# Second cross-attention and feed-forward of a two-block transformer: program order in one pool, inverses by way of DRAM, one row spread to 64 partitions by each transfer

## The chip, the cores and the metric

The kernel runs on one core of a Trainium2 chip. TensorE (PE) multiplies matrices into PSUM; VectorE (DVE), ScalarE (ACT) and GpSimd (POOL) do elementwise work; SyncE (SP), and ACT in a few places, issue DMA transfers. Each engine executes its own instructions in order and waits on semaphores for the others. The metric is device time in microseconds of one execution, lower is better.

## The reference

Two blocks work on x of shape 8 x 512 x 256 (batches, tokens, features), all in float32, with a conditioning vector per batch and 64 context tokens of 192 features per batch. The first block has a self-attention with 16 heads of 16, a cross-attention and a gated feed-forward. The second block, cut to what matters here:

```python
attn_in = adaln(x, cond, ...)                  # layer norm, then (1+g) and b from cond
x = attn(attn_in, attn_in, sa_wq, sa_wkv, sa_wo, sa_bo) + x     # 16 heads of 64
cross_in = adaln(x, cond, ...)                 # the same g and b as above
x = attn(cross_in, layernorm(context), ca_wq, ca_wkv, ca_wo, ca_bo) + x
ffn_in = adaln(x, cond, ...)
x = gelu(ffn_in @ ff_w1 + ff_b1) @ ff_w2 + ff_b2 + x            # 256 -> 1024 -> 256
```

`attn` projects queries, keys and values, rotates queries and keys (RoPE), takes softmax(q k / 8) v for each head and projects by the output matrix.

## The kernel before, in words

All eight batches' x stay in SBUF, 128 tokens to a partition group, four groups to a batch. The program runs in phases; this change touches the last three, those of the second block.

*Self-attention (pool `ph4`).* Its order on PE, DVE, ACT and POOL is the order in which the code is written (`manual_schedule`). For each batch there are four groups of four heads, and for each group four slots, one for each 128 keys: `score` multiplies and ACT takes the exponential, `value` multiplies by v one slot later. POOL and DVE add the exponentials over the key tiles (`sm`). At the end of a group `sums` adds them over partitions by matmuls; ACT copies the denominators, they go to DRAM and come back as 128 x 16 (`sums_back`); `inverse` takes the reciprocal on DVE and writes it to DRAM; `inverse_back` (L950) reads two rows at a time to 128 partitions, each to 64, and `scaled` (L955) multiplies the head outputs `oT`. `out_tiles` projects them. These transfers go by SP, those of the last group of the last batch by ACT. In that last group's tail the values of the cross-attention (`cross_values`, eight matmul pairs, ACT copies v, SP writes it to DRAM in `v_d`) fill PE between the steps of the inverses. A batch takes 123.7 us.

*Cross-attention (pool `ph5`).* Here the framework's scheduler sets the order on each engine, from the dependences and the order of the code as priority; it can also move work up between instructions of the phase before. Each batch has eight pairs of heads and four blocks of two pairs. `norm` makes the normed rows, transposes them (L366, eight 128 x 128 transposes and two ACT copies) and adds the output bias to x (POOL, L380). `context` loads the batch's keys and values from DRAM into block-diagonal tiles `kb` and `vb` (six transfers). `outer` multiplies values by the output matrix beforehand, giving `vw`. `queries` multiplies, and `rope_pair` rotates: DVE at L720 and twice at L723, POOL adds at L724. `score` multiplies two pairs into one tile of two PSUM banks, and ACT takes the exponential to `p`. After four blocks, `sums` adds over the keys into one bank; DVE takes the reciprocal there of 128 x 512 (L1091), four transfers write the 16 needed rows to DRAM (L1095), and eight transfers (L1101) spread them, each two rows to 64 partitions; POOL and DVE in turn multiply `p` by them (L1104). Two blocks later the projection of `p` by `vw` adds to x.

*Feed-forward (pool `ph6`).* Also in the scheduler's order. The rows of each batch are normed and transposed; `ff_w1` in 32 matmuls (L1155 has the GELU on ACT), `ff_w2` in 64, DVE adds to x (L396), and SP stores the batch. Before the first batch a check over all reciprocals (`chk`, collected by `check`, L150) is reduced to one flag `good`, by which a general path is taken if the fast one is not safe.

*PSUM.* Eight banks: two tiles `S` of two banks each, two `X`, one `O`, one `D`. `bank_x` gives every third tile from `D` in the first block; from the second block's self-attention on (`turns.clear()`) it gives only the two `X`.

*What a norm is.* `layernorm` takes statistics on DVE (L187, L188; four pairs a batch), POOL raises to the power -1/2 (L179), DVE scales (L191).

All matmuls stand under line 107, in the helper `mm`; each of the program's float32 matmuls is two instructions in the trace.

Of the kernel before, what the change touches and what calls it, by code (L numbers as in the profile page):

```python
# [18 lines left out]
P = 128  # L19
# [59 lines left out]
def fast_path(ctx: ExitStack, tc: tile.TileContext, a: dict, out: bass.AP):  # L79
# [8 lines left out]
    turns = [0]  # L88
# [10 lines left out]
    def bank_x():  # L99
        if turns:  # L100
            turns[0] += 1
            if turns[0] % 3 == 0:
                return bank_d()
        return psum.tile([P, 512], F32, tag="X", name="ps_X", bufs=2)

# [268 lines left out]

    def normed_T(pool, x, b, eps, am, bm, bufs=2):
        return transposed(pool, normed(pool, b, eps), b, am, bm, bufs)
# [335 lines left out]
    k_d = dram.tile([B, P, NPAIR, T], F32, name="k_d", bufs=1)  # L712
    v_d = dram.tile([B, P, NPAIR, T], F32, name="v_d", bufs=1)
# [23 lines left out]
    def keys1(p):  # L737
# [6 lines left out]
        nc.sync.dma_start(k_d[:, :, p, :].rearrange("b r t -> r b t"), q.rearrange("p (b t) -> p b t", b=B))  # L744
# [56 lines left out]
    turns.clear()  # L801
# [9 lines left out]
    def load_kb(b):  # L811
        for i in range(4):
            r = slice(32 * i, 32 * i + 32)
            nc.sync.dma_start(kvs[b % 2][0][r, :, i % 2, :], k_d[b, r])

    def load_vb(b):
        for e in range(2):
            r = slice(64 * e, 64 * e + 64)
            nc.sync.dma_start(kvs[b % 2][1][r, :, e, :], v_d[b, r])
# [5 lines left out]
    def cross_values(wk, p):  # L825
        ps = bank_x()
        for k in range(2):
            mm(ps, cross["v"][:, k, p * P : (p + 1) * P], ctxzT[:, k, :], k == 0, k == 1)
        v = wk.tile([P, N], F32, tag="k0", name="v")
        nc.scalar.copy(v, ps)  # L830
        nc.sync.dma_start(v_d[:, :, p, :].rearrange("b r t -> r b t"), v.rearrange("p (b t) -> p b t", b=B))


    with tc.tile_pool(name="ph4", bufs=2) as wk:
        NG = H // 4
        kb, vb = kv_first()
        steps, mid = {}, {}
# [4 lines left out]
        def batch4(b):  # L842
# [103 lines left out]
            def inverse_back(g):  # L946
                d = s["inv", g]
                for u in range(2):
                    s["rb", g, u] = rb = wk.tile([P, N], F32, tag="rb", name="rb", bufs=3)
                    queue(g).dma_start(rb, d[2 * u : 2 * u + 2, None, :].to_broadcast([2, 64, N]))  # L950
# [51 lines left out]
        def slots():  # L1002
# [14 lines left out]
            sums(NG - 1)  # L1017
            for p in range(NPAIR):
# [4 lines left out]
            load_vb(0)  # L1023
            for qp in range(2):
# [5 lines left out]
    w_co, w_cq, rope_s2 = cross["o"], cross["q"], cross["s"]  # L1030


    with tc.tile_pool(name="ph5", bufs=2) as wk:
        kvs.append(tuple(wk.tile([P, NPAIR, 2, T], F32, name=n, bufs=1) for n in ("kb", "vb")))
        for z in kvs[1]:
            nc.gpsimd.memset(z, 0.0)

        w_f1 = load_w("ff_w1", 1)
        w_f2 = load_w("ff_w2", 3)
        blocks = []  # L1040

        def batch5(b):
            s = {}

            def norm():
                s["hT"] = transposed((nk, wk)[b % 2], normed(nk, b, EPS1), b, a1, b1, 1)
                add_row(b, row("cabo"))

            def context():
                s["kb"], s["vb"] = kvs[b % 2]  # L1050
                if b:
                    load_kb(b)
                    load_vb(b)

            def outer(pp):

                if pp == 0:
                    s["vw"] = wk.tile([P, NPAIR, D], F32, tag="vw", name="vw", bufs=3)
                ps = bank_x()
                for i in range(2):  # L1060
                    p = 2 * pp + i
                    mm(ps[:, i * D : (i + 1) * D], s["vb"][:, p, :, :].rearrange("p e k -> p (e k)"), w_co[:, p, :])
                nc.scalar.copy(s["vw"][:, 2 * pp : 2 * pp + 2, :], ps.rearrange("p (i d) -> p i d", i=2))

            def queries(p):
                ps = bank_x()
                for k in range(2):
                    mm(ps, w_cq[:, k, p * P : (p + 1) * P], s["hT"][:, k, :], k == 0, k == 1)
                s[p] = q = wk.tile([P, N], F32, tag="q", name="q", bufs=6)
                rope_pair(wk, ps[:, None, :], rope_c[:, None, :], rope_s2[:, None, :], [P, 1, N], q[:, None, :])  # L1070

            def block(pp):
                def score():
                    ps = bank_s()
                    for i in range(2):
                        p = 2 * pp + i
                        mm(ps[:, i, :], s["kb"][:, p, :, :].rearrange("p e k -> p (e k)"), s[p])
                    s["p", pp] = wk.tile([P, 2, N], F32, tag="p", name="p", bufs=8)
                    nc.scalar.activation(s["p", pp], ps, AF.Exp, scale=HD1 ** -0.5)

                return Block([score], [])

            def sums():

                d = bank_d()
                for i in range(2):
                    for j in range(4):
                        p = 4 * i + j
                        mm(d[32 * j : 32 * j + 32, :], sel3[:, i, :], s["p", p // 2][:, p % 2, :], i == 0, i == 1)
                rec = wk.tile([P, N], F32, tag="rec", name="rec", bufs=1)  # L1090
                nc.vector.reciprocal(rec, d)  # L1091
                rd = dram.tile([NPAIR, 2, N], F32, tag="rec5", name="rec5")
# [934 lines left out]
```

## Time and profile before

| | us |
|---|---|
| median of 3 runs (2522.51 to 2525.21) | 2523.86 |
| the profiled execution's own time | 2522.38 |
| its span, first to last instruction | 2520.5 |
| PE busy in the span | 2437.0 (97%) |
| DVE, ACT, POOL busy | 1095.1, 871.3, 850.9 |
| first matmul of the cross-attention after the last output tiles of the self-attention | 1907.3 |
| feed-forward's first matmul | 2281.1 |

The span is that of the profiled execution. Times in the text are microseconds from its start. "PE busy" counts a matmul from its start to the modelled end of its pipeline, so that consecutive ones overlap. A wait in square brackets behind an instruction is the time that its engine was idle before it, and the instruction that ended this. A transfer is issued by an engine's queue (SPq, ACTq) and lands later; the chain of waits shows transfers under DMA.

### The profile page before, as it was taken

To read this page: it belongs to the slowest core of one execution; us is meant where nothing else is said; L and a number is where in the kernel's file an instruction comes from. 1 tells how busy PE (TensorE), PEld (TensorE's weight loads), DVE (VectorE), ACT (ScalarE), POOL (GpSimd) and SP (SyncE) were. 2 spreads that over 40 slices of the span, in tenths; PEclk is the share of its full clock that TensorE was granted. 3 is DMA by queue.
4 is the path that set the end of the run, shared out by engine and by line. 5 is a ranking of instruction groups with operands and counts; after the bars stand their busy time and mean duration, and the time that the engine had idled before them with its cause. 6 is when DMAs were issued, how large, how long until landed. Compare 5 with 4: busy or idle time off the path is not lost.

```text
span 2520.5 us, 27970 instructions
## 1 busy us (share of the span) xinstructions
PE 2437.0 (97%) x10938; PEld 1152.9 (46%) x10938; DVE 1095.1 (43%) x2039; ACT 871.3 (35%) x1099; POOL 850.9 (34%) x521
## 2 busy tenths in 40 slices
PE   8999999999999899999999999999989999999999
PEld 3333443443445533434343434343435456556665
DVE  4555435435435334343444434445326765652000
ACT  3555546545542133242424243333232111112221
POOL 3453222322300035353535353536324434431000
PEclk9999999999999999999999999999999999999999
DMA  5130000000002000000000000000131321320000
GB/s 180 35 95 9 16 17 10 16 11 12 12 11 88 0 4 28 18 18 18 19 18 18 18 18 18 18 18 18 51 92 40 79 49 42 76 68 9 17 17 26
DMA packets 91084, 83.76 MB, mean 33 GB/s; under 512 B 51104, under 2 KB 67424, under 8 KB 90936
## 3 DMA queue, kind: packets, MB, share of 16 engines
q1 hardware_dynamic: 90388, 81.34, 11.0%
q8 instruction: 88, 1.44, 0.2%
q10 hardware_dynamic: 556, 0.55, 0.1%
q14 instruction: 52, 0.43, 0.1%
HBM read 72.09 MB, written 9.77 MB: 32 GB/s over the span
## 4 chain that ended last, share of the span: by engine, by line
PE 87%; DVE 4%; DMA 3%; issue 2%; POOL 2%; ACT 2%; SPq 0%; DVEq 0%; POOLq 0%; ACTq 0%
PE ps_X L107 42%; PE ps_S L107 22%; PE ps_D L107 11%; PE ps_O L107 9%; PE ps_X L366 1%; DMA rb<-rec_d 1%; DVE t L723 1%; ACT p L505 1%; POOL q L724 1%; DMA rb<-rec 1%; DVE t L720 1%; DVE st L187 1%; PE ps_X L485 0%; POOL p L1104 0%; PE ps_X L527 0%
## 5 line engine op out<-in xcount | busy, mean ns | idle before, releaser
L107 PE MATMUL ps_S<-q,k 32*128 32x512 f32 (+1 forms) x3072 | 432.5, 628 | 7.0 <-ACT p L505 3.4
L892 ACT ACTIVATE p<-ps_S 128x1024 f32<-128x1024 f32 x256 | 248.4, 1022 | 526.6 <-PE ps_S L107 519.1
L505 ACT ACTIVATE p<-ps_S 128x1024 f32<-128x1024 f32 x256 | 248.2, 1022 | 259.7 <-PE ps_S L107 258.8
L107 PEld LDWEIGHTS ps_S<-q,k 32*128 32x128 f32 (+1 forms) x3072 | 160.6, 185 | 245.7 <-issue 136.4
L871 DVE TENSOR_TENSOR t<-ps_X,rope_c 128x512 f32<-128x512 f32 x126 | 87.1, 691 | 341.0 <-PE ps_X L107 341.0
L911 DVE TENSOR_TENSOR sm<-sm,p 128x1024 f32<-128x1024 f32 x128 | 192.3, 1546 | 55.6 <-ACT p L892 54.3
L396 DVE TENSOR_TENSOR x<-ps_X,x 128x512 f32<-128x512 f32 x48 | 33.2, 692 | 342.6 <-PE ps_X L107 342.6
L874 POOL TENSOR_TENSOR q<-t 128x512 f32<-128x512 f32 x32 | 40.7, 1273 | 384.2 <-DVE t L872 384.2
L107 PE MATMUL ps_X<-hT,w 128*128 128x512 f32 x344 | 160.6, 601 | 1.6 <-DVE t L678 1.1
L907 POOL TENSOR_TENSOR sm<-p 128x1024 f32<-128x1024 f32 x64 | 149.2, 2353 | 32.5 <-ACT p L892 32.5
L724 POOL TENSOR_TENSOR q<-t,t 128x512 f32<-128x512 f32 x72 | 97.2, 1353 | 159.0 <-DVE t L723 151.3
L107 PE MATMUL ps_O<-p,h 128*32 128x512 f32 x1024 | 138.1, 612 | 0.5 <-ACT oT L518 0.5
L107 PE MATMUL ps_O<-p,v 128*64 128x512 f32 x512 | 138.0, 617 | 0.0
L107 PE MATMUL ps_D<-p,v 128*64 128x512 f32 x512 | 131.6, 592 | 1.1 <-ACT p L892 1.1
L179 POOL TENSOR_TENSOR rstd<-rstd,mhalf 128x4 f32<-128x4 f32 x49 | 49.6, 1015 | 241.4 <-DVE rstd L178 239.3
L107 PE MATMUL ps_X<-vw,p 128*128 128x256 f32 x512 | 119.2, 389 | 10.9 <-DVE p L1104 9.8
L107 PE MATMUL ps_X<-w_sa_wo,oT 128*128 128x256 f32 x512 | 118.0, 389 | 11.2 <-DVE oT L955 6.4
L380 POOL TENSOR_TENSOR x<-x,rows 128x1024 f32<-128x1024 f32 x24 | 56.5, 2354 | 196.9 <-DVE z L191 195.4
L107 PE MATMUL ps_X<-hT,w_sa_wq 128*128 128x512 f32 x256 | 115.9, 595 | 4.2 <-ACT hT L367 4.2
L107 PE MATMUL ps_X<-w_sa_wv,hT 128*128 128x512 f32 x256 | 118.0, 604 | 0.0
L107 PE MATMUL ps_S<-hT,w_ff_w 128*128 128x512 f32 x256 | 117.9, 604 | 0.1
L107 PE MATMUL ps_X<-hT,w_ca_wq 128*128 128x512 f32 x256 | 117.3, 598 | 0.7 <-DVE t L723 0.7
(219 smaller groups left out, 3546.4 us busy)
## 6 DMA issues: line engine op xcount, KB each, us to landing
rb<-rec SPq DMA_DIRECT2D x80, 256.0 KB
rb<-rec_d SPq DMA_DIRECT2D x62, 256.0 KB
x<-in_x_dram SPq DMA_DIRECT2D x8, 512.0 KB
out_dram<-x SPq DMA_DIRECT2D x8, 512.0 KB
bc<-modd SPq DMA_DIRECT2D x8, 384.0 KB
gate<-modd SPq DMA_DIRECT2D x16, 128.0 KB
k_d<-q SPq DMA_DIRECT2D x8, 256.0 KB
v_d<-v SPq DMA_DIRECT2D x8, 256.0 KB
```

What stands on the lines that cost most here:

```text
L107: nc.tensor.matmul(o, lhsT, rhs, start=start, stop=stop)
L179: nc.gpsimd.tensor_tensor(r[:, :n], r[:, :n], mhalf[:, :n], ALU.pow)
L187: nc.vector.bn_stats(st[:, t, :], src[:, t, :])
L380: nc.gpsimd.tensor_tensor(xs[b], xs[b], r[:, None, :].to_broadcast([P, NT, D]), ALU.add)
L396: nc.vector.tensor_tensor(x, ps, x, ALU.add)
L505: nc.scalar.activation(pr[u], pss[u], AF.Exp, scale=HD0 ** -0.5)
L724: nc.gpsimd.tensor_tensor(dst, t1, t2, ALU.add)
L871: nc.vector.tensor_tensor(c, ps, rope_c, ALU.mult)
L874: nc.gpsimd.tensor_tensor(r[0], ec, os, ALU.subtract)
L892: nc.scalar.activation(pr, pss[u], AF.Exp, scale=HD1 ** -0.5)
L907: nc.gpsimd.tensor_tensor(sm, s["p", g, 0, u], s["p", g, 1, u], ALU.add)
L911: nc.vector.tensor_tensor(s["sm", g, u], s["sm", g, u], s["p", g, t, u], ALU.add)
```

## The change

- The second cross-attention and the feed-forward stand in one pool and in the order of the code on PE, DVE, ACT and POOL (`cross`, `feed_forward`). Queries run three pairs ahead (`LEAD`). A batch has eight steps j. Each even step has a score; its outputs are projected in the next batch's steps 4 to 7, those of the last batch in the feed-forward after its first four `up`. The norm of a batch is taken at step 5 two batches ahead, its transposes at step 4 one batch ahead. The first batch's norm and transposes move into the self-attention's tail.
- The cross-attention's denominators are copied by ACT, go to DRAM in four transfers and come back as 128 x 64; DVE takes the reciprocal of that (step 1 of the next batch), it goes to DRAM, and sixteen transfers (step 3) spread one row each to 64 partitions; `rb` has four buffers of one pair in place of two buffers of two pairs, and POOL and DVE take pairs in turn.
- In the self-attention, too, each transfer spreads one row to 64 partitions: four for a group in place of two.
- `bank_x` has `D` and `O` as well as the two `X` in these last phases, in rotation.
- `k_d` and `v_d` lie in DRAM with the partition outermost, so that a pair's write is one run of 2 KB a partition; the reads take runs of 256 bytes. `v` has four buffers in place of two.
- `hid` has one buffer. The flag is made after the second batch of the feed-forward. Each batch is stored in two halves.

```diff
+    extra.append(bank_d)
+        n = turns[0] % (2 + len(extra))
+        if n < len(extra):
+            return extra[n]()
...
-    k_d = dram.tile([B, P, NPAIR, T], F32, name="k_d", bufs=1)
+    k_d = dram.tile([P, NPAIR, B, T], F32, name="k_d", bufs=1)
...
-                    queue(g).dma_start(rb, d[2 * u : 2 * u + 2, None, :].to_broadcast([2, 64, N]))
+                    for e in range(2):
+                        queue(g).dma_start(rb[64 * e : 64 * e + 64, :],
+                                           d[2 * u + e : 2 * u + e + 1, :].to_broadcast([64, N]))
...
             sums(NG - 1)
+            first_rows.append(normed(nk, 0, EPS1))
+            add_row(0, row("cabo"))
...
             load_vb(0)
+            first_rows.append(transposed(nk, first_rows[0], 0, a1, b1, 1))
             for qp in range(2):
                 out_tiles(qp)
...
+        def sums(b):
...
+            nc.scalar.copy(den, d)
+            dd = dram.tile([NPAIR, 2, N], F32, tag="den5", name="den5")
+            for i in range(2):
+                for e in range(2):
+                    nc.sync.dma_start(dd[4 * i : 4 * i + 4, e, :], den.rearrange("(j r) n -> j r n", j=4)[:, 2 * i + e, :])
+            s["rec"] = rec = wk.tile([P, H * N // P], F32, tag="rec", name="rec", bufs=1)
+            nc.sync.dma_start(rec, flat(dd))
+
+        def inverse(b):
...
+            nc.vector.reciprocal(rec, rec)
+            rd = dram.tile([NPAIR, 2, N], F32, tag="rec5", name="rec5")
+            nc.sync.dma_start(flat(rd), rec)
+            check(rec)
...
+        def scaled(b):
+            s = ss[b]
+            for p in range(NPAIR):
+                rb = wk.tile([P, N], F32, tag="rb", name="rb", bufs=4)
+                for e in range(2):
+                    nc.sync.dma_start(rb[64 * e : 64 * e + 64, :], s["rd"][p, e : e + 1, :].to_broadcast([64, N]))
+                pr = s["p", p // 2][:, p % 2, :]
+                (nc.gpsimd, nc.vector)[p % 2].tensor_tensor(pr, pr, rb, ALU.mult)
...
+        def cross():
+            LEAD = 3
+            for n in range(LEAD):
+                queries(n)
+            for z in kvs[1]:
+                nc.gpsimd.memset(z, 0.0)
+            for b in range(B):
+                for j in range(NPAIR):
+                    if j % 2 == 0:
+                        score(b, j // 2)
+                    if j == 6 and b:
+                        cross_out(b - 1, 2)
+                    queries(NPAIR * b + j + LEAD)
+                    if (b, j) == (0, 1):
+                        rows_(1)
+                    if j < 2:
+                        outer(b, 2 * j)
+                        outer(b, 2 * j + 1)
+                    if b:
+                        if j == 1:
+                            inverse(b - 1)
+                        if j == 3:
+                            scaled(b - 1)
+                        if j in (4, 5, 7):
+                            cross_out(b - 1, j - 4)
+                    if j == 2 and b + 1 < B:
+                        load_kb(b + 1)
+                        load_vb(b + 1)
+                    if j == 4:
+                        turn(b + 1)
+                    if j == 5:
+                        rows_(b + 2)
+                    if j == 7:
+                        sums(b)
+
+        def feed_forward():
+            good = None
+            for b in range(B):
+                for ff in range(4):
+                    up(b, ff)
+                    if b == 0 and ff == 1:
+                        inverse(B - 1)
+                    if b == 0 and ff == 3:
+                        scaled(B - 1)
+                if b == 0:
+                    for t in range(4):
+                        cross_out(B - 1, t)
+                turn(B + b + 1)
+                for t in range(4):
+                    down(b, t)
+                    if t == 1:
+                        rows_(B + b + 2)
+                if b == 1:
+                    good = within()
+            return good
+
+        with tc.manual_schedule(engines={ENG.PE, ENG.DVE, ENG.Activation, ENG.Pool}):
+            cross()
+            return feed_forward()
```

## The prediction

> **What bounds the kernel now.** I read first the busy times by stretch (microseconds from the start of the span; columns: length, then PE, PEld, DVE, ACT, POOL busy with instruction counts, clock, DMA share, GB/s):
>
> ```profile
> 1588.00:1712.00 124.00, 123.38 (x585) 52.82 (x584) 58.22 (x118) 42.26 (x54) 53.71 (x37) 1.00 0.05 17
> 1712.00:1836.00 124.00, 120.28 (x556) 51.00 (x560) 52.39 (x76) 41.77 (x53) 55.82 (x36) 0.99 0.14 41
> 1836.00:1907.00 71.00, 57.08 (x246) 28.67 (x243) 15.31 (x20) 18.20 (x25) 11.75 (x8) 0.88 0.27 76
> 1907.00:2000.00 93.00, 85.70 (x282) 43.90 (x281) 68.48 (x107) 20.68 (x27) 46.82 (x32) 1.00 0.27 63
> 2093.00:2185.00 92.00, 87.25 (x303) 50.61 (x302) 57.70 (x88) 15.77 (x20) 38.23 (x24) 0.98 0.24 58
> 2279.00:2396.00 117.00, 116.40 (x420) 74.23 (x419) 21.00 (x49) 29.98 (x43) 14.80 (x8) 1.00 0.04 14
> ```
>
> TensorE (PE) sets the pace throughout: self-attention (to 1836) and feed-forward (from 2279) have it busy nearly always. The changed code starts at the end of self-attention. What can be won there is PE's idle time: 14 us in 1836 to 1907, some 5 to 7 us per 93 in the cross-attention, almost nothing after. Next, the PE timeline at the first of these places:
>
> ```profile
> 1877.23 2.75 PE L107 MATMUL ps_X<-w_sa_wo,oT 128*128 128x256 f32 x12
> 1884.86 1.22 PE L107 MATMUL ps_X<-w_sa_wo,oT 128*128 128x256 f32 x2 [4.88 <-POOL oT L955]
> 1892.45 13.57 PE L107 MATMUL ps_X<-w_sa_wo,oT 128*128 128x256 f32 x50 [6.36 <-DVE oT L955]
> 1907.32 1.13 PE L107 MATMUL ps_X<-w_ca_wo,kv 128*128 128x256 f32 x4
> ```
>
> and the chain of waits, which says what the multiplies by the inverses (L955) waited for; two lines stand for the two ways of spreading inverses, that of the self-attention (rec_d) and that of the cross-attention (rec):
>
> ```profile
> 1874.72 16.88 DMA rb<-rec_d
> ...
> 2254.60 3.71 DMA rb<-rec
> ```
>
> The windows 1841:1849 and 2239:2243, each inside a run of such transfers, show the difference:
>
> ```profile
> 1841.00:1849.00 8.00, 8.00 (x54) 2.57 (x50) 0.11 (x1) 5.42 (x7) 1.27 (x1) 1.00 0.13 50
> 2239.00:2243.00 4.00, 4.00 (x11) 1.39 (x9) 1.34 (x2) 1.50 (x2) 2.45 (x3) 1.00 1.05 244
> ```
>
> Two rows to 128 partitions in one transfer, outermost size 2, keep an eighth of the DMA engines busy (0.13: two of 16) at 50 GB/s; 64 partitions outermost keeps all busy at 244.
>
> **The change, part by part.** The sum is made against the profiled execution, 2522.4 us (span 2520.5); it lies 1.5 under the median 2523.86.
>
> *1. Last self-attention group.* Each transfer now spreads one row to 64 partitions. I take the 3.7 us of the cross-attention's form instead of 16.88. The inverses leave at 1874.1 (four issues of 0.32 to 0.53 on ACT) and land by about 1879.5. The output tiles need the late pairs only as the seventh and eighth of eight operands, 2.6 us in, so neither wait of 4.88 and 6.36 remains. Batch 0's eight transposes (1.1 us and a bank copy, 0.78) now stand ahead of these tiles: they start at 1878.9, take 64 x 0.216 = 13.8 (rate below) and end at 1892.7. Before, the same point is 1907.3. **-14.6.** The values' rows go out as 2 KB pieces through four buffers where ACT waited 9.1 us for a v buffer; that wait goes too, but it lay beside PE's waits and is not counted again. Late next would be POOL's add of a 128x1024 row (2.36), which ends before the inverses land. In earlier groups PE does not wait on rb, so four issues for two cost nothing there (SP is idle for most of each 31 us group).
>
> *2. Norms hoisted by the scheduler.* The last batch of self-attention repeats the one before with the same matmuls, but with 3.1 us more PE idle and a stretch at half clock. The DVE groups from 1690 to 1730 show why:
>
> ```profile
> L187 DVE BATCH_NORM_STATS2 st<-x 128x6 f32<-128x256 f32 x28 | 10.4, 398 | 0.0
> ```
>
> A batch has 4; the 24 others belong to the second cross-attention and were moved up. In program order they cannot be. **-4.1** (matmul 540 of the batch comes at 119.82 us instead of 115.76).
>
> *3. Cross-attention.* The rates, from runs of back-to-back matmuls: 512 columns 0.43 us (28 in 12.64), 256 columns 0.216 (64 in 13.82):
>
> ```profile
> 2413.41 13.82 PE ps_X L107 x64
> 2427.23 12.64 PE ps_S L107 x28
> 2440.65 1.98 PE ps_S L107 x4
> ```
>
> A batch has 32 of the first for queries (13.8), 16 for scores (6.9), 16 of the second for vw (3.45) and 64 for outputs (13.8), transposes 1.1, sums 1.85: 40.9 of PE. Before, eight batches took 1907.3 to 2279.1: 371.8, or 46.5 each. Does program order get nearer to 40.9? The path of one query is
>
> ```profile
> 1942.48 3.60 PE L107 MATMUL ps_X<-hT,w_ca_wq 128*128 128x512 f32 x8
> 1944.47 0.69 DVE L720 TENSOR_TENSOR t<-ps_X,rope_c 128x512 f32<-128x512 f32 x1 [2.29 <-PE ps_X L107]
> 1945.18 1.39 DVE L723 TENSOR_TENSOR t<-ps_X,rope_s 64x512 f32<-64x512 f32 x2
> 1946.71 1.28 POOL L724 TENSOR_TENSOR q<-t,t 128x512 f32<-128x512 f32 x1 [3.13 <-DVE t L723]
> ```
>
> 0.27 + 2.1 + 0.13 + 1.28 + 0.06 = 3.8 us from PE's end to the score. Count from the end of the previous sums. Step j=4's score needs query 5, ending at 12.0, with one query (1.72) between: PE waits 2.1. The denominators now go ACT copy, four transfers (0.5 each, 1.7 to land), one back: there at 6. But their reciprocal stands on DVE behind query 4's rotation, which ends at 9.2; it takes 0.5 (128x32 took 0.343, 128x512 3.358). On SP the inverses' write is followed by the six loads of the next keys and values (2.54 and 1.28 now), so the spreads begin at 13.9. Sixteen for eight: one row to 128 partitions (bc) takes 0.32 to issue where rb takes 0.60, so 5.1 us for 4.8; with 0.55 apiece it would be 8.8. A pair lands 3.3 to 3.5 after its start (a single 256 KB one: 3.5 to 3.7) and pairs follow each other by 1.17 (the landings at 2241.11, 2242.30, 2243.47). With four rb buffers the fifth pair waits for the first multiply, on POOL (1.27; DVE 0.69), which itself queues behind query 6 until 17.8. The eighth multiply is done between 25.5 and 26.8, and the first output tile ends at 26.0 to 27.3 instead of 20.65. Behind those multiplies on DVE waits query 7's rotation (2.1), and for its bank the next batch's first query: 0.6. A batch is 46.8 to 48.1, I take 47.4. The DVE reciprocal of 3.36 and the two checks of 0.65 on 512 columns go, but DVE is not PE's limit here. Batch 0 has no outputs: 32.2 of work with three leading queries. The first score waits 2.5: these queries take PE 5.2, but DVE turns them at 2.1 each from 2.0 on, and POOL has the second at 7.65. Query 5 waits behind batch 1's norm on DVE (5.0: statistics 2.2, POOL's power and its handovers 1.3, four scalings 1.5) and POOL's row add (2.36): ready at 25.5 where PE is at 21.4, 4.2 with the handover. The next norm costs 3.7 in the same way before batch 1's first score, and bank copies and query 7 0.9: 43.5. The last batch has no successor's queries: 41.6. Its outputs, now in the feed-forward, take 13.8; nothing stands ahead of reciprocal and spreads there (from 6 and 8.3), so the eighth multiply is done at 20 to 20.7 where PE would be at 17.2 less one operand: 3.7 of wait. Sum: 43.5 + 6 x 47.4 + 41.6 + 17.5 = 387.0. **+15.2.**
>
> *4. Clock.* Idle of 1.98 us at 2075.9 was followed by 3.4 us at half clock; the window 2075:2083 has
>
> ```profile
> 2075.00:2083.00 8.00, 6.02 (x19) 4.26 (x18) 6.09 (x7) 0.00 (x0) 1.26 (x1) 0.79 0.29 77
> ```
>
> while 2.79 us at 2247 was not. Each halving costs up to 1.7. Between 0 and 12 for seven batches; much would fall inside the wait for inverses, so I take **+3.5**.
>
> *5. Feed-forward.* The period is 29.3: 13.8 down, the rest 14.6 up and transposes. In program order 13.8 + 13.8, transposes 1.1: 8 x 27.6 + 7 x 1.1 = 228.5 against 2279.1 to 2514.3. **-6.7.** One hid buffer suffices, since a GELU (0.69) follows its own matmul. The closing check moves beside matmuls with DVE nearly idle. The last store is half as large: **-0.5.** Keys' and values' layouts move pieces of 256 bytes from the write to both ends of the read, where they were already 256 bytes at the destination: nothing.
>
> Sum: -14.6 - 4.1 + 15.2 + 3.5 - 6.7 - 0.5 = -7.2, so 2515.2, and 2517 on the median's scale.
>
> Two rules of the Trainium skill speak against parts of this. "DMA: Bandwidth & Descriptors", Rules for kernel authors, advises against two transfers to disjoint partition halves, for one to all 128; by it term 1 would be 0 and the total +7.4. The windows of 50 and 244 GB/s show the one transfer as the slow one here, and the same table explains it by the outermost size. "TensorE: Matmul & The Clock Gate", Why this matters for your kernels, names idle gaps over some 3 us as what drops the clock; by it most of term 4 would vanish and the total be -10.7. The 1.98 us above contradicts it.
>
> **The rivals.** *The inverses arrive in time (faster still).* If the eighth multiply were done by 20, a batch costs 40.9 + 2.1 + 0.6 = 43.6; seven save 27, and the clock term falls: about 2487 to 2500. For it: DMA queues near empty. Against: six loads ahead on SP and four buffers.
> *The wait for inverses outweighs the rest (slower).* Place: output tile 0 at j=4. Every microsecond more costs 7; from 48.4 per batch (first output ending at 27.7) the change gains nothing. At 49.5 with half clock after every wait: 7 x 2.1 + 5 above my sum, 2537. For it: issues at 0.55, landings behind the loads. Against: the spreading was measured at 1.17 a pair.
> *The two sides cancel.* A batch of 47.7 to 49.1 leaves the time within 5 us: about 2523.
> *The spread is no faster than now* (a row with stride 0 served by few engines): term 1 vanishes, and 7 us or more is lost; unlikely, since 64 partitions outermost ran at 244. It is counted with the slower rival.
>
> **How the numbers follow.** Forecast (46 to 47.7 per batch; own range 2505 to 2519) 0.42; in time 0.14; cancel 0.20; slower 0.24. A measurement can tell about 0.2%, 5 us. So faster 0.56, same 0.20, slower 0.24. The range leaves out the lower part of the second case and the upper of the last: 2495 to 2537.
>
> **What would show it.** Right: no PE wait on oT after 1877; 4 stats in the last self-attention batch; PE waits on multiplied p once a batch, 4 to 7 us in all with the query's 2.1; a feed-forward period of 28.7. Wrong: a cross-attention period under 45 or over 48.4, PE waiting on a bank or on a rotation elsewhere, or spreads landing more than 1.2 us apart.

## The result, and the profile after

| | before | after |
|---|---|---|
| median of the runs, us | 2523.32 | 2561.97 |
| their range | 2522.51 to 2525.21 | 2556.66 to 2568.52 |
| profiled execution; its span | 2522.38; 2520.5 | 2558.11; 2556.3 |

The ratio is 1.0153 (interval 1.0125 to 1.0182): the changed kernel is 38.6 us slower. The prediction was 2517, with a range of 2495 to 2537. The table sets the two profiled executions against the prediction's terms. The feed-forward is counted as the prediction counted it: before, from its first transposes at 2279.1 (its first matmul is at 2281.1); after, where its transposes stand in the cross-attention, from its first matmul at 2274.7; in both to the end of its last matmul. The predicted times are those of before plus the terms named.

| part | before | predicted | after | error |
|---|---|---|---|---|
| start to first matmul of the cross-attention (terms 1, 2) | 1907.3 | 1888.6 | 1882.8 | -5.8 |
| cross-attention, to the start of the feed-forward (terms 3, 4) | 371.8 | 373.0 | 391.8 | +18.8 |
| feed-forward, with the last batch's outputs (term 5, and 17.5 of term 3) | 235.2 | 246.0 | 276.2 | +30.2 |
| rest, to the execution's own time | 8.1 | 7.6 | 7.3 | -0.3 |

The last batch's outputs stand in the second row before and in the third after, so only the sum of both rows compares before with after: +61.0, where +12.0 was predicted. In the same order of stretches as before, the windows of the changed kernel (columns as there: length, then PE, PEld, DVE, ACT, POOL busy, clock, DMA share, GB/s):

```profile
1712.00:1836.00 124.00, 124.00 (x597) 52.61 (x597) 45.97 (x63) 42.46 (x53) 49.29 (x33) 1.00 0.15 44
1836.00:1907.00 71.00, 66.97 (x260) 34.36 (x256) 30.05 (x59) 20.84 (x30) 27.37 (x19) 1.00 0.31 90
2093.00:2185.00 92.00, 83.36 (x283) 49.57 (x282) 44.55 (x81) 14.77 (x19) 34.75 (x26) 0.91 0.19 52
2279.00:2396.00 117.00, 105.69 (x385) 69.22 (x384) 21.14 (x60) 22.00 (x32) 15.15 (x10) 1.00 0.10 32
```

The first two have become better: PE is busy for all of the last self-attention batch (120.28 before) and for 67 of the next 71 us (57.08 before). The last two have become worse: in the cross-attention PE is busy for less of the time and at a clock of 0.91, and in the feed-forward, which had PE busy for 116.40 of 117 us, it is idle for 11. The waits of PE from 1836 on name the causes (us in total, times, longest):

```profile
PE ps_S L109 <- ACT hid L1146: 25.1, 32, 0.9
PE ps_S L109 <- POOL q L723: 15.0, 11, 3.1
PE ps_X L109 <- POOL p L1124: 11.8, 12, 2.3
PE ps_D L109 <- POOL p L1124: 9.4, 8, 2.0
PE ps_O L109 <- POOL p L1124: 8.9, 6, 3.0
```

The first line has no counterpart in the prediction at all. It is a wait for the GELU of the feed-forward (`hid`), 32 times 0.78 us. The other four were foreseen in kind: a wait for a rotated query and waits for multiplied `p`. Together they are 45.1 us, 5.6 a batch; the prediction named 4 to 7, but with one wait for `p` a batch, and there are 26 in seven batches.

The tail of the self-attention on PE's timeline (start, us, idle before in brackets) has neither wait on `oT` left, and the 64 matmul instructions of the output tiles stand in one run:

```profile
1868.90 14.08 PE L109 MATMUL ps_X<-w_sa_wo,oT 128*128 128x256 f32 x64
1882.82 1.88 PE L109 MATMUL ps_O<-hT,w_ca_wq 128*128 128x512 f32 x4
```

One batch of the cross-attention, from the score of its third block to its first output tile (the sums before it ended at 2075.70):

```profile
2091.63 1.12 PE L109 MATMUL ps_S<-q,kv 128*128 128x512 f32 x2 [1.11 <-POOL q L723]
...
2094.96 1.25 PE L109 MATMUL ps_X<-vw,p 128*128 128x256 f32 x4 [0.48 <-POOL p L1124]
2097.33 1.85 PE L109 MATMUL ps_X<-vw,p 128*128 128x256 f32 x4 [1.12 <-POOL p L1124]
2099.82 2.18 PE L109 MATMUL ps_X<-vw,p 128*128 128x256 f32 x4 [0.64 <-POOL p L1124]
2102.46 2.07 PE L109 MATMUL ps_X<-vw,p 128*128 128x256 f32 x4 [0.46 <-POOL p L1124]
```

The output tile trickles: PE gets two of the eight pairs of heads (four instructions) at a time and waits for the next. The last three of these lines also show the clock. The same four instructions that take 1.03 us in a dense run (1.25 here at 2094.96) take 1.85 to 2.18. The granted clock (third column from the end) is 0.50 from there to behind the tile:

```profile
2098.00:2107.00 9.00, 7.88 (x20) 4.83 (x20) 3.46 (x5) 1.50 (x2) 3.79 (x3) 0.50 0.24 78
```

What feeds this tile stands on SP's queue (its issues of the same stretch):

```profile
2085.60 0.33 SPq L1113 DMA_DIRECT2D rec<-rec  x1
2085.98 0.59 SPq L818 DMA_DIRECT2D kv<-v_d  x1
2089.43 10.42 SPq L1122 DMA_DIRECT2D rb<-rec  x16
```

and on DVE:

```profile
2085.02 0.55 DVE L1111 RECIPROCAL rec<-rec 128x64 f32<-128x64 f32 x1
...
2100.03 0.69 DVE L1124 TENSOR_TENSOR p<-p,rb 128x512 f32<-128x512 f32 x1 [2.21 <-DMA rb<-rec]
2102.39 0.69 DVE L1124 TENSOR_TENSOR p<-p,rb 128x512 f32<-128x512 f32 x1 [1.67 <-DMA rb<-rec]
```

The sixteen spreads take SP 10.4 us to issue, and seven of the eight multiplies wait for their transfer. In the next batch, whose sums end at 2126.37, the spreads begin 1.8 us sooner after the sums and take longer:

```profile
2138.32 12.64 SPq L1122 DMA_DIRECT2D rb<-rec  x16
```

They end 24.6 us after the sums there, and 24.1 in the batch above. The first eight are out after 5 us; then SP waits for the first multiply to free one of the four buffers. Four more of the seven batches with a successor go like this one.

The feed-forward, two `up` steps in a row:

```profile
2456.35 3.70 PE L109 MATMUL ps_S<-hT,w_ff_w 128*128 128x512 f32 x8 [0.78 <-ACT hid L1146]
2460.83 3.70 PE L109 MATMUL ps_S<-hT,w_ff_w 128*128 128x512 f32 x8 [0.78 <-ACT hid L1146]
```

Eight instructions and a wait of 0.78: a step takes 4.48 us, where eight of them at the prediction's rate (0.43) are 3.44; 32 such steps make 33 us. An `up` computes two 512-column halves in one PSUM tile `ps`. The code issues the matmuls of half 0, its GELU on ACT, the matmuls of half 1, its GELU. The matmuls of half 1 write the tile that the first GELU reads; in the order of the code they come behind it, and they wait. (Each line above begins with the second half of one `up`.)

### The profile page after: what moved, and what is told of

Its sections match the earlier page's. It is cut to its first block, busy times and chain, and to the rows that moved or that the text cites. A ratio compares the mean times of both kernels' runs of the same rounds, so it can differ in the third digit from the quotient of the medians.

```text
span 2556.3 us, 28290 instructions
## 1 busy us (share of the span) xinstructions
PE 2442.8 (96%) x10938; PEld 1160.8 (45%) x10938; DVE 1059.9 (41%) x2055; ACT 877.2 (34%) x1107; POOL 854.2 (33%) x537
## 4 chain that ended last, share of the span: by engine, by line
PE 87%; DMA 3%; DVE 2%; ACT 2%; POOL 2%; SPq 2%; issue 1%; POOLq 0%; DVEq 0%; ACTq 0%
PE ps_X L109 35%; PE ps_S L109 22%; PE ps_D L109 15%; PE ps_O L109 13%; DMA rb<-rec 2%; SPq L1122 2%; PE ps_X L368 1%; POOL p L1124 1%; ACT p L504 1%; ACT hid L1146 1%; DMA rec<-rec 1%; DVE t L722 1%; PE ps_X L484 0%; ACT hT L369 0%; PE ps_X L526 0%
## 5 line engine op out<-in xcount | busy, mean ns | idle before, releaser
L504 ACT ACTIVATE p<-ps_S 128x1024 f32<-128x1024 f32 x256 | 248.2, 1022 | 258.3 <-PE ps_S L109 257.4
L723 POOL TENSOR_TENSOR q<-t,t 128x512 f32<-128x512 f32 x72 | 92.0, 1279 | 200.5 <-DVE t L722 193.0
L395 DVE TENSOR_TENSOR x<-ps_X,x 128x512 f32<-128x512 f32 x26 | 18.0, 692 | 228.9 <-PE ps_X L109 228.9
L109 PE MATMUL ps_X<-hT,w_sa_wk 128*128 128x512 f32 x248 | 112.4, 596 | 0.0
L1146 ACT ACTIVATE hid<-ps_S,cols 128x512 f32<-128x512 f32 x64 | 44.0, 687 | 193.4 <-PE ps_S L109 193.4
L475 POOL TENSOR_TENSOR rstd<-var,mhalf 128x32 f32<-128x32 f32 (+1 forms) x17 | 87.3, 5134 | 68.2 <-ACT t L676 41.7
```

What stands on the lines that cost most here:

```text
L109: nc.tensor.matmul(o, lhsT, rhs, start=start, stop=stop)
L475: nc.gpsimd.tensor_tensor(r, s["var", c][:, :, hd], half, ALU.pow)
L504: nc.scalar.activation(pr[u], pss[u], AF.Exp, scale=HD0 ** -0.5)
L723: nc.gpsimd.tensor_tensor(dst, t1, t2, ALU.add)
L1146: nc.scalar.activation(s["hid"][:, f, :], ps[:, i, :], AF.Gelu, bias=col("ffb1")[:, f : f + 1])
```

## The experiments

The period of the cross-attention below is the time from one batch's sums to the next one's, taken over the second to the seventh batch; that of the feed-forward is the time from one batch's first `up` to the next.

**1. The GELU behind both halves.** In `up` of the changed kernel, both GELUs are issued after all four matmuls (eight instructions).

```diff
                 for k in range(2):
                     mm(ps[:, i, :], w_f1[...], turned_rows[B + b][:, k, :], k == 0, k == 1)
+            for i in range(2):
+                f = 2 * ff + i
                 nc.scalar.activation(s["hid"][:, f, :], ps[:, i, :], AF.Gelu, ...)
```

> The changed kernel, but in the feed-forward both GELUs of a two-bank PSUM tile are issued after all eight matmuls into it, not one after each half. Theory (the second half's matmuls wait for the first half's GELU, since the order of the code is now the order of the engines and the two halves are one tile): the 0.78 us of PE idle behind each first GELU goes, an `up` pair takes 3.45 instead of 4.48, 32 of them: about 31 us less, 2527 to 2531. Rival (the feed-forward is slow for another reason: one hid buffer, the stores in halves, the transposes): no more than 5 us less, 2553 to 2562.

Measured 2537.31 us, ratio to the kernel before 1.0053 (1.0037 to 1.0070), 24.7 us under the changed kernel. The 32 matmul instructions of `ff_w1` now stand in one run on PE's timeline:

```profile
2446.26 13.90 PE L109 MATMUL ps_S<-hT,w_ff_w 128*128 128x512 f32 x32
```

The feed-forward's period falls from 32.6 to 28.4, which over eight batches is 33.6 us. It also confirms the 28.7 that the prediction had for a feed-forward in program order without such a wait. The kernel gains less than 33.6 and than the 31 expected: 24.7 by the medians, 20.0 in the two profiled executions. In the profiled one the cross-attention starts 2.5 us later and takes 5.4 us longer, in its first two batches; why was not studied. And the first feed-forward period, which holds the last cross-attention batch's outputs, is 1.4 us longer and not 4.2 shorter: behind the shorter `up` these outputs wait 3.2 us for `p`, where they had no wait in the changed kernel. The kernel is still 0.5% slower than before: the rest is the cross-attention, where the period is 51.0, as in the changed kernel (50.9).

**2. The new spread alone.** The kernel before, with only the one-row transfers in the self-attention.

```diff
-                    queue(g).dma_start(rb, d[2 * u : 2 * u + 2, None, :].to_broadcast([2, 64, N]))
+                    for e in range(2):
+                        queue(g).dma_start(rb[64 * e : 64 * e + 64, :],
+                                           d[2 * u + e : 2 * u + e + 1, :].to_broadcast([64, N]))
```

> The kernel before, with one part of the change alone: in the self-attention each transfer spreads one row to 64 partitions, four for a group in place of two. Theory (this edit alone made the tail of the self-attention faster, by the landing of the inverses, 20 us in the changed kernel beside the 4 us of the hoisted norms): 2503 to 2510, and the first matmul of the cross-attention's values about 14 to 20 us earlier than 1907. Rival (the gain in the changed kernel came from the first batch's norm and transposes standing ahead of the output tiles, or from the v buffers): 2517 to 2523.

Measured 2508.92 us, ratio 0.9935 (0.9916 to 0.9954). The output tiles of the last batch follow the values without a wait:

```profile
1870.09 14.00 PE L107 MATMUL ps_X<-ctxzT,w_ca_wvp 96*128 96x512 f32 x32
1884.03 14.25 PE L107 MATMUL ps_X<-w_sa_wo,oT 128*128 128x256 f32 x64
```

Counted from the first query of the self-attention, the last of these matmuls starts 17.2 us earlier than in the kernel before; in the changed kernel 21.6 us earlier. The 4.4 us between the two are what the changed kernel gains otherwise. The norm statistics that are no longer moved up agree with that: in the last self-attention batch (1712 to 1836) PE is busy for 120.08 us here, as before (120.28), and for 124.00 in the changed kernel, and in the DVE groups between 1690 and 1836 this kernel (first line) still has 32 statistics, the changed kernel (second line) 4. No run has that part alone.

```profile
L187 DVE BATCH_NORM_STATS2 st<-x 128x6 f32<-128x256 f32 x32 | 11.9, 401 | 0.1
```

```profile
L189 DVE BATCH_NORM_STATS2 st<-x 128x6 f32<-128x256 f32 x4 | 1.6, 400 | 0.0
```

So the new spread is a gain of 14 us by itself (12 to 21 by the interval), and the prediction's first two terms stand.

**3. Matmuls that nobody needs in place of the wait.** Experiment 1's kernel, with ten extra matmuls of 256 columns (0.43 us each, 4.3 a batch) between the operands of the first output tile, into a spare bank that nobody reads. All that is computed otherwise stays.

```diff
+            spare = bank_s() if b < B - 1 else None
+            for k in range(8):
+                if b < B - 1:
+                    filler(spare[:, 0, 0:D], {0: 2, 2: 2, 4: 4, 6: 2}.get(k, 0))
+                mm(s["ps"][:, 0:D], s["p", k // 2][:, k % 2, 0:P], s["vw"][:, k, :], k == 0, k == 7)
```

> e1_gelu_behind, with ten idle matmuls of 256 columns (0.43 us each, 4.3 us a batch) put between the operands of each batch's first output tile, into a spare bank that nobody reads, where PE waits for the inverses. Theory (the wait there drops TensorE's clock to half for 7 to 10 us of each batch, and 2 to 3 us of that fall behind the wait): the half-clock stretches shrink, a cross-attention batch takes 48 to 49 instead of 51, the kernel 10 to 20 us less than e1_gelu_behind, although PE does 30 us more work. Rival (the clock is low only while PE waits anyway): the same as e1_gelu_behind or slower by up to 10 us.

Measured 2523.13 us, ratio 1.0002 (0.9993 to 1.0012): 14.2 us *less* than experiment 1 with 30 us *more* of PE's work. Two batches of experiment 1 and the same two here, by windows:

```profile
1990.00:2092.00 102.00, 91.00 (x306) 53.45 (x305) 53.55 (x93) 17.32 (x23) 38.30 (x28) 0.93 0.19 54
```

```profile
1985.00:2083.00 98.00, 91.93 (x342) 56.68 (x341) 51.81 (x92) 16.95 (x22) 38.10 (x28) 1.00 0.19 56
```

The clock is 1.00 instead of 0.93, and the period 49.4 instead of 51.0. The inverses come as late as before: the first output tile still waits for them between the extra matmuls. So 1.6 us of a batch is the lower clock. That the rest is the lateness is left to experiment 8.

**4. The changed kernel's steps in the scheduler's order.** The cross-attention and the feed-forward of the changed kernel, their transfers and buffers included, without the hand-set order.

```diff
-        with tc.manual_schedule(engines={ENG.PE, ENG.DVE, ENG.Activation, ENG.Pool}):
-            cross()
-            return feed_forward()
+        cross()
+        return feed_forward()
```

> The changed kernel, but the cross-attention and the feed-forward are again ordered by the framework's scheduler, with all else as changed (one pool, inverses by way of DRAM, four banks in rotation). Theory (program order costs the feed-forward some 30 us by the GELU wait and the cross-attention some 4 us a batch): the feed-forward period back at 29.3 and the whole at 2505 to 2530. Rival (the inverses' way through DRAM and the sixteen spreads are what costs the cross-attention, in any order): a cross-attention batch of 50 or more, the whole at 2530 to 2545.

Measured 2501.02 us, ratio 0.9910 (0.9890 to 0.9930). That is under both ranges. The period of the cross-attention is 46.6 (50.9 in the changed kernel) at a clock of 1.00, that of the feed-forward 29.3. The inverses are not earlier: the last multiply by them ends 29 to 34 us after the sums, in the first seven batches, later than in the changed kernel (27 to 31). But the scheduler has put queries and scores between the operands of the output tile:

```profile
2081.03 0.70 PE L109 MATMUL ps_X<-vw,p 128*128 128x256 f32 x2 [1.13 <-DVE p L1124]
2081.56 1.02 PE L109 MATMUL ps_X<-hT,w_ca_wq 128*128 128x512 f32 x2
2082.42 1.02 PE L109 MATMUL ps_S<-q,kv 128*128 128x512 f32 x2
2085.33 0.70 PE L109 MATMUL ps_X<-vw,p 128*128 128x256 f32 x2 [1.89 <-POOL p L1124]
```

Sixteen one-row spreads and the way through DRAM are therefore not by themselves what makes the changed kernel slow; the order of the steps is. Experiments 5 and 8 ask which steps.

**5. The inverses earlier and the outputs later, within a batch.** Experiment 1's kernel with four queries ahead, reciprocal and first four pairs of spreads in step 0, the multiplies two pairs a step in steps 2 to 5, and the outputs in steps 5, 6, 7 and 7.

```diff
-            LEAD = 3
+            LEAD = 4
...
-                        if j == 1:
+                        if j == 0:
                             inverse(b - 1)
-                        if j == 3:
-                            scaled(b - 1)
-                        if j in (4, 5, 7):
-                            cross_out(b - 1, j - 4)
+                            spreads(b - 1, range(4))
+                        if 2 <= j <= 5:
+                            scaled(b - 1, {2: (0, 1), 3: (2, 3), 4: (4, 5), 5: (6, 7)}[j])
+                        if j in (5, 6):
+                            cross_out(b - 1, j - 5)
+                        if j == 7:
+                            cross_out(b - 1, 2)
+                            cross_out(b - 1, 3)
```

> e1_gelu_behind with the cross-attention's program order changed and nothing else: queries run four pairs ahead in place of three, the reciprocal and the first four spreads stand in step 0 of the next batch, the multiplies go two pairs a step from step 2 to 5 with the last four spreads behind the first four multiplies, the transposes in step 3, and the outputs in steps 5, 6, 7 and 7 in place of 4 to 7. Theory (a batch takes 51 instead of 40.9 us because the output tiles stand before the inverses can be there, and TensorE's clock falls in that wait): a batch of 41 to 44, no half-clock stretch in most batches, 2465 to 2490. Rival (program order itself, or sixteen transfers a batch on SP, keeps a batch at 46 or more wherever the outputs stand): 2500 to 2540.

Measured 2513.47 us, ratio 0.9965 (0.9954 to 0.9976). The period is 49.9 where 41 to 44 was expected; period and time lie in the rival's ranges. The kernel is 23.8 us under experiment 1; by the traces only 5.7 of that lie between the sums of the second and the seventh batch, the rest in the first two batches and the last. The first spread is issued 1.7 us earlier after the sums than in experiment 1, but the sixteen take SP 13.83 us, where they take 12.65 there, and PE waits at the same place (timeline of SP, then of PE):

```profile
2078.97 13.83 SPq L1122 DMA_DIRECT2D rb<-rec  x16
...
2090.46 1.13 PE L109 MATMUL ps_X<-vw,p 128*128 128x256 f32 x4 [0.85 <-POOL p L1128]
2093.35 1.13 PE L109 MATMUL ps_X<-vw,p 128*128 128x256 f32 x4 [1.76 <-POOL p L1128]
2097.43 1.90 PE L109 MATMUL ps_X<-vw,p 128*128 128x256 f32 x4 [2.95 <-POOL p L1128]
```

There are four buffers for the spread rows. Pairs five to eight can be issued only as the first four are multiplied, and these multiplies now stand on DVE and POOL between the rotations of queries. The last one ends 28.6 us after the sums, as late as ever.

**6. Half as many transfers.** Experiment 1's kernel with two rows of a parity in one transfer of 256 KB, eight for sixteen, into two buffers of two pairs: the same memory.

```diff
-            for p in range(NPAIR):
-                rb = wk.tile([P, N], F32, tag="rb", name="rb", bufs=4)
+            for pp in range(4):
+                rb = wk.tile([P, 2, N], F32, tag="rb", name="rb", bufs=2)
                 for e in range(2):
-                    nc.sync.dma_start(rb[64 * e : 64 * e + 64, :], s["rd"][p, e : e + 1, :].to_broadcast([64, N]))
+                    nc.sync.dma_start(rb[64 * e : 64 * e + 64, :, :],
+                                      s["rd"][2 * pp : 2 * pp + 2, e, :][None].to_broadcast([64, 2, N]))
```

> e1_gelu_behind, but in the cross-attention a transfer spreads two rows to 64 partitions (64 outermost), eight transfers of 256 KB a batch in place of sixteen of 128 KB, two buffers of two pairs. Theory (sixteen issues of 0.59 us on SP, 10 us a batch, set the pace of the spreads): eight issues take 5 us, the last multiply of a batch ends about 2 us sooner after the reciprocal, a batch takes 48.5 to 50, 2523 to 2532. Rival (buffers and landings set it): within 4 us of e1_gelu_behind.

Measured 2540.42 us, ratio 1.0063 (1.0045 to 1.0081), against 1.0053 for experiment 1: no gain. SP's eight issues are themselves 4.8 us, but spread over 10.60, for the second half waits for buffers, and the multiplies wait for that half (timeline of SP, then two lines of DVE):

```profile
2100.89 10.60 SPq L1122 DMA_DIRECT2D rb<-rec  x8
...
2107.98 1.15 DVE L1126 TENSOR_TENSOR p<-p,rb 128x512 f32<-128x512 f32 x1 [0.52 <-DMA rb<-rec]
2113.40 0.69 DVE L1126 TENSOR_TENSOR p<-p,rb 128x512 f32<-128x512 f32 x1 [4.27 <-DMA rb<-rec]
```

The last multiply ends 28.5 to 28.9 us after the sums in the second to the seventh batch, no sooner than in experiment 1 (27.7 to 28.0). So the number of issues is not the limit by itself. The chain of buffer, transfer and multiply, in two turns, is at least as long. A kernel with eight buffers was not run.

**7. Only the cross-attention in the scheduler's order.** Experiment 1's kernel, with `cross()` outside the hand-set order.

```diff
+        cross()
         with tc.manual_schedule(engines={ENG.PE, ENG.DVE, ENG.Activation, ENG.Pool}):
-            cross()
             return feed_forward()
```

> e1_gelu_behind, but the cross-attention ordered by the framework's scheduler; the feed-forward stays in program order with both GELUs behind the matmuls. If program order was a loss for the cross-attention alone and is a gain for the feed-forward (28.4 a batch against the scheduler's 29.3): 2492 to 2500, 4 to 8 us under e4_auto. If the scheduler's gain in e4_auto came from moving feed-forward matmuls up into the last batches' waits, which this kernel cannot do: 2500 to 2512.

Measured 2503.76 us, ratio 0.9918 (0.9893 to 0.9944), the same as experiment 4 within the intervals. It lies in the range of the second forecast, but the trace doesn't show the reason given there: the first two feed-forward batches, where experiment 4 moves matmuls up ahead of the last outputs, take 78.4 us here and 78.1 there. The feed-forward's period is 28.4 instead of 29.3 after that. Against it, the period of the cross-attention is 48.1 (46.6 in experiment 4), at a mean clock of 0.97 (1.00); why was not studied. The last batch's outputs, behind the first four `up` by the order of the code, wait 3.5 us in all for their operands.

**8. The outputs behind the next batch's sums.** In nearly all batches of the kernels so far the last multiply ends 27 to 35 us after the sums, so here the outputs are moved to where that doesn't matter. This is experiment 5's kernel with a batch's four output tiles after the sums of the next batch, with the reciprocal and two queries between them. They are the last readers of `p` before the batch after that overwrites it, so no buffer is added.

```diff
+                    if j == 0 and b:
+                        for t in range(4):
+                            if b > 1:
+                                cross_out(b - 2, t)
+                                if t % 2 == 0:
+                                    queries(NPAIR * b + t // 2 + LEAD)
+                            if t == 1:
+                                inverse(b - 1)
+                                spreads(b - 1, range(4))
...
-                        if j in (5, 6):
-                            cross_out(b - 1, j - 5)
-                        if j == 7:
-                            cross_out(b - 1, 2)
-                            cross_out(b - 1, 3)
...
         def feed_forward():
+            for t in range(4):
+                cross_out(B - 2, t)
+                if t == 1:
+                    inverse(B - 1)
+                    spreads(B - 1, range(4))
```

> The order of e6_reordered with the four output tiles of a batch moved behind the sums of the next batch, that is some 40 us after their own sums (the last multiply ends 28 to 29 us after the sums in every ordered kernel so far). If the lateness of the inverses is what is left of the cross-attention's idle time, PE waits on no multiplied p, a batch takes 41 to 44 us in place of 49.5 to 51, little half clock is left, and the kernel ends near 2470 (2460 to 2485), below the version with the scheduler's order (2501). Rival: the rotations on DVE (8 x 2.1, with norm and multiplies some 24 us in the 27 us between the outputs) or the waits for banks set the pace; then a batch stays at 46 to 49 and the kernel ends between 2495 and 2515.

Measured 2466.47 us (2465.84 to 2467.32), ratio 0.9781 (0.9763 to 0.9798): 2.2% faster than the kernel before, 47.0 us under experiment 5, and the fastest version here. The period is 43.2. PE's waits from 1836 to the end no longer have a line for `p`:

```profile
PE ps_D L109 <- DVE t L722: 5.6, 3, 1.9
PE ps_X L109 <- DVE t L722: 3.7, 2, 1.9
PE ps_O L109 <- DVE t L722: 3.7, 2, 1.9
PE ps_S L109 <- POOL q L723: 1.8, 1, 1.8
```

and the outputs on the timeline, behind the sums (`sel`), are dense:

```profile
2030.81 1.92 PE L109 MATMUL ps_D<-p,sel 128*32 128x512 f32 x16
2032.66 3.72 PE L109 MATMUL ps_O<-vw,p 128*128 128x256 f32 x16
2038.27 3.05 PE L109 MATMUL ps_X<-hT,w_ca_wq 128*128 128x512 f32 x4 [1.88 <-DVE t L722]
2041.11 4.26 PE L109 MATMUL ps_O<-vw,p 128*128 128x256 f32 x16
```

The inverses are not earlier: in the second to the sixth batch the last multiply ends 43.6 to 45.3 us after its sums, later than in any kernel above and just behind the next sums, but the outputs now stand late enough for that. The kernel keeps the order of the code and the sixteen spreads, so neither holds a batch at 46 or more, as the rival of experiment 5 had it. What is left is one wait of 1.9 a batch, for a rotation that frees a bank, in the one query between the first two tiles. Its idle time is again followed by half clock in this batch (the query's four instructions take 3.05 for 1.88).

## Why the prediction was wrong

Of the 42.9 us between the predicted 2515.2 and the profiled 2558.1, the feed-forward's row has 30.2 and the cross-attention's 18.8; the first row takes 5.8 back.

*Term 1 (inverses of the last self-attention group, -14.6): right.* Neither wait on `oT` is left, and experiment 2 gives 17.2 by the trace and 14.0 us by the medians.

*Term 2 (norms moved up, -4.1): right.* PE is busy for 124.00 of 124 us, 4 statistics instead of 32, and 4.4 us lie between experiment 2 and the changed kernel, though no run isolates the norms.

*Term 3 (cross-attention, 47.4 a batch): the mechanism right, the size wrong.* The place was the one named, output tile 0, and the period of 50.9 is over the 48.4 that was to show the prediction wrong. The reciprocal came when it was due, 9.3 us after the sums (9.2 predicted). So did the first spread in the batch shown, 13.7 (13.9), but by luck: of the six loads said to be ahead on SP only one, of 0.59, stands between the write of the inverses and the spreads, the four of the keys come behind the spreads, and SP issues nothing from 2086.6 to 2089.43. In five of the seven batches the first spread goes out at 11.4 to 12.0. The issue of a spread was mis-sized: I took 0.32, from a row to 128 partitions (`bc`), and set aside 0.55. It is 0.594, as much as the spread of the kernel before (0.60), the nearer row:

```profile
L1122 SPq DMA_DIRECT2D rb<-rec x128: 444/594/598, 1935.7 to 2292.2; - x128
```

Sixteen then take 9 us of SP's time instead of 5.1. But that is not what fixes the end, for in the five batches SP stops for some 3 us after the first eight, and issues the ninth at 19.7, when the first pair's multiply has ended and freed a buffer. That multiply starts at 17.9 to 18.4, behind query 6, nearly as predicted (17.8). The step that failed is the time from there to the eighth multiply: 7.7 to 9.0 predicted, 9.4 to 10.0 measured from the second batch on. The last four pairs go out 1.25 apart, two issues each (1.17 predicted), and the last pair's multiply starts 3.6 to 3.8 after its first issue (3.3 to 3.5 predicted for the landing). The eighth multiply ends 27.4 us after the sums in the batch shown, predicted 25.5 to 26.8, and the first output tile ends 28.8 after them, predicted 26.0 to 27.3, its last four instructions at half clock. That is 1.5 to 2.8 late. With the clock kept at 1.00 by experiment 3, a batch takes 49.4, 2.0 more than predicted. Experiment 6 shows that fewer issues alone do not mend it.

*Term 4 (clock, +3.5 in all): mechanism right, size wrong.* Experiment 3 puts it at 14.2 us even with the extra work counted in, above the 0 to 12 that I allowed. I argued from one gap of 1.98 us that one halving of 3.4 us would follow a wait, and that much of it would fall inside the wait. In fact four short waits per tile, of 0.5 to 1.1 us each, kept PE at half clock through most of the tile and some us behind it: the mean clock over the cross-attention is 0.93. The rule of the Trainium skill that I weighed ("TensorE: Matmul & The Clock Gate", Why this matters for your kernels: idle gaps over some 3 us drop the clock) would have made most of this term vanish; here no single gap in the batch shown is over 1.2 us, and the clock fell all the same.

*Term 5 (feed-forward, -6.7): wrong, and the largest error (+30.2).* The step that failed is the sum 13.8 + 13.8 + 1.1: it puts matmuls back to back and the wait for the GELU at nothing. "A GELU (0.69) follows its own matmul" was used only to say that one `hid` buffer suffices, and I did not ask what stands between the matmuls in the code's order. The GELU of half 0 stands between the halves of one PSUM tile, a wait of 0.78 us 32 times, 4.2 us a batch by experiment 1's period. Experiment 1 shortens this row of the table from 276.2 to 248.2, so 28.0 of the 30.2 are this wait. PE has no wait on `hid` in the kernel before, nor in experiment 4, both in the scheduler's order. No rival held this mechanism. Without the wait the period of 28.7 was right (28.4).

*The rivals.* "The wait for inverses outweighs the rest", at 49.5 a batch with half clock after every wait, is in kind what happened in the cross-attention, at 50.9 a batch. It was priced at 2537, and experiment 1, which has that and not the GELU's wait, measures 2537.31. So near a value is luck: by experiment 1's trace the cross-attention takes 24.3 us more than predicted, where this rival added 19.7, and it starts 3.2 us sooner. "The inverses arrive in time" never came about by faster inverses. Experiment 8 comes to 43.2 a batch, where this rival had 43.6, by a later use of them. The advice of the Trainium skill against two transfers to disjoint halves ("DMA: Bandwidth & Descriptors", Rules for kernel authors) would have made term 1 zero; experiment 2, 14.0 us faster by two such transfers in place of one, decides for the row of the trace.

## What to carry to other kernels

When work goes from a scheduler's order into the order of the code, sum not only the instructions: go through each engine's sequence once for every pair of writer and reader of the same buffer, and ask what stood between them before. Two halves of one PSUM tile are one buffer in this code. And where a result comes late by a chain of transfers, moving its consumer by half a batch can be worth much more than shortening the chain: here 47 us, where halving the number of transfers gained nothing.

## What the runs showed of the hardware

- A trickle of matmuls can hold the clock down without a long gap. In the changed kernel, waits of 0.46 to 1.12 us between runs of four matmuls go with runs of 1.85 to 2.18 us, for 1.03 in a dense run. The granted clock is 0.50 from 2098 to 2107 there. Filling the waits with 4.3 us of useless matmuls a batch made experiment 1's kernel 14.2 us faster.
- The time to issue a transfer on SP depends on its shape. In the median one row to 64 partitions takes 0.594 us, one row to 128 partitions 0.318 (the eight `bc` transfers of the kernel before); the write of 128 x 64 inverses takes 0.33.
- Two 128 KB spreads of one row to 64 partitions are much quicker than one 256 KB transfer of two rows with outermost size 2: exchanging the one for the others took 17.2 us off the path behind the last group of the self-attention.
